# Layer norm, attention and feed-forward on one core: the kernel's own planner lays its steps out in parts, with nine tries for each

## The chip, the cores and the metric

The kernel runs on one core of a Trainium2 chip. A core has five engines that run their own instruction streams in order and meet through semaphores: TensorE (PE) for matrix products, VectorE (DVE), ScalarE (ACT) and GpSimd (POOL) for element work, and SyncE (SP), which here issues most of the DMAs. The metric is the device time of one execution in microseconds, the median of the runs shown.

## The reference

For 16 sequences of 512 tokens with 512 features, a layer norm feeds two branches, and both are added to the input:

```python
xn = _layernorm(x, axis=-1)
x = x + _L0_attn_ref(xn, w_qkv, b_qkv, w_out, b_out) + _L0_ffn_ref(xn, gate_w, up_w, down_w, gate_s, up_s, down_s)

# attention: 16 heads of 32, causal
qkv = einsum('bsd,ed->bse', x, w_qkv) + b_qkv
scores = einsum('bhqd,bhkd->bhqk', q, k) / sqrt(32) + causal
out = einsum('bhqk,bhkd->bhqd', softmax(scores), v)
return einsum('bsd,ed->bse', out, w_out) + b_out

# feed-forward: 1408 inner features, ternary weights with a scale for each row
g = einsum('th,ih->ti', xf, gate_w) * gate_s
u = einsum('th,ih->ti', xf, up_w) * up_s
return einsum('ti,hi->th', silu(g) * u, down_w) * down_s
```

## The kernel before

All is in float32 outside, and inside the operands of the large products are split into a high and a low float16 half (`xh` and `xl`, `qkh` and `qkl`, `hh` and `hl`, `oh` and `ol`), so that a product is made of two or three float16 products. The ternary weights of the feed-forward are held in fp8.

One batch is one sequence. Its heads come in four groups of four; a slot is one group of one batch, so there are 64 slots. For a slot PE makes the query and key projections (`qk`), the scores (`s`, L726) in runs, and the weighted sum of the values (`av`, L867). A run of scores fills the four PSUM banks of tag `s1`: run "3" has the last 128 queries against 512 keys, run "2, 0" the third and the first, run "1, 1" the second blocks of two slots. Names such as `s1_13` mean slot 1, block 3. For each of the four heads of a run DVE takes the row maximum with the mask (L765), ACT the exponential with its sum (L770); then ACT and DVE make the two halves `pq` (L797, L802), and a transposing DMA on SP's queue brings them to `pT` for the values product. The next run needs the four banks back, so it waits for the exponentials of the run before.

All other products of PE go through `mm_group` (one line, L359) in pieces of four matmuls of 512 columns, into three PSUM banks of tag `mm`: gate `g`, up `u`, down `dn`, `qk`, `v` and the output projection `op`. They fill the time between the score runs. Gate and up are evicted by ACT (tanh, L947), DVE (L951, L957), ACT again (`hh`, L960) and POOL (`hl`, L961).

The layer norm of the next batch runs beside this: four statistics steps on DVE (L484, L485), a seed of the inverse deviation on DVE (L491, L43, L44), Newton's steps on POOL (`newton_steps`, L50 to L53, twelve small operations, planned as one step of 2.9 us), the normalisation on DVE (`ln_norm`, L509, four steps planned at 0.5 us each), the high half on ACT (L522), the low half on POOL (L523), and transposing DMAs. DVE also carries small tests of the weights that are spread over the batches (L1046, L1053). At the end of the last batch, `av_step` with `split` makes the last slot's values product in two halves (`av`, `av_first`), each followed by its own eviction (L882, L900, L905), and the output products of the last group come after it.

Nothing of this is issued in the order in which it is written. Each piece is a `Step` with an engine, a duration estimated by hand, a latency, the tokens that it reads and writes, and for PE a key (where in the whole it should stand). `Plan.order` at the kernel's end lays all steps out in time, on the host, and the engines' streams are then issued in that order. Before the change it works so:

- `layout` goes from start to end. For each engine it lists the steps that can begin, with their start times; PE takes the earliest (among equals one that keeps the array's mode, then the smallest key), the others the earliest, and among equals the one with the smallest deadline `late`. If taking it would make a more urgent step late that comes free within WINDOW = 0.5 us, they wait for that one. The earliest choice over all engines is put into the plan.
- A change between wide, row-tiled and column-tiled products on PE costs SWITCH = 0.095 us in the layout.
- `deadlines` goes back through a finished layout and gives each step its latest end, from what needs it, from the buffer that it keeps, and for PE from its place in a row of PE steps without gaps.
- `order(6)` does this six times and takes the layout that ends first.

Of the kernel before, what the change touches and what calls it, by code (L numbers as in the profile page):

```python
# [2 lines left out]

# [54 lines left out]
SWITCH, LANDING = 0.095, 1.4  # L58
WINDOW = 0.5

BEGIN, FIRST_TURN = 0.75, 1.3

RUNS = 0.0, 0.17, 0.30, 0.64, 0.80
LAST_RUNS = 0.0, 0.14, 0.28, 0.42, 0.56
VERBOSE = False


# [26 lines left out]
class Plan:  # L94
# [30 lines left out]
        self.steps.append(st)  # L125
        return st

    def order(self, times):


        for n, st in enumerate(self.steps):
            st.n = n
            for d in st.deps:
                d.next.append(st)
        best = None
        for _ in range(times):
            done = self.layout()
            if done is None:
                break
            end = max(st.end for st in done)  # L140
            if best is None or end < best[0]:
                best = end, done, [(st.start, st.end) for st in done]
            if VERBOSE: print("pass", end)
            self.deadlines(done)
        for st, (t0, t1) in zip(*best[1:]) if best else ():
            st.start, st.end = t0, t1
        assert best, "no step can start"
        return best[1]

    def tiles(self):  # L150
        return dict.fromkeys(t for st in self.steps for t in st.tiles)
# [1 line left out]
    def deadlines(self, done):  # L153
        rings = {}
        for t in self.tiles():
            rings.setdefault(t.tag, {})[t.index] = t
        after = {}
        for ring in rings.values():
            for k, t in ring.items():
                if k >= t.bufs:  # L160
                    first = min(t.users, key=lambda u: u.start)
                    for u in ring[k - t.bufs].users:
                        after.setdefault(u, []).append(first)
        total, at = max(st.end for st in done), {}
        t = next(st.start for st in done if st.eng == "PE")
        for st in done:
            if st.eng == "PE":
                at[st] = t
                t += st.dur
        for st in done[::-1]:  # L170
            late = [x.late - st.lat * (x.eng != st.eng or st.dma) for x in st.next]
            late += [x.late - st.lat for x in after.get(st, ())]
            spent = st.lat + LANDING if st.dma else st.dur
            st.late = min([total] + late) - spent
            if st.eng == "PE":
                st.late = min(st.late, at[st])

    def layout(self):
        for st in self.steps:
            st.left, st.end = len(st.deps), None  # L180
            for t in st.tiles:
                t.index = None
        free = dict.fromkeys(self.ENGINES, BEGIN)
        ready = {e: [] for e in self.ENGINES}
        made, done, dma, mode = {}, [], FIRST_TURN, "wide"
        keys = sorted((s.key, s.n) for s in self.steps if s.eng == "PE")[::-1]

        def begin(st):

            t, more = st.at, {}  # L190
            if st.behind and st.behind.end is None:
                return None
            for b in st.tiles:
                if b.index is None:
                    l = made.setdefault(b.tag, [])
                    k = len(l) + more.get(b.tag, 0) - b.bufs
                    more[b.tag] = more.get(b.tag, 0) + 1
                    if k >= 0:
                        for u in l[k].users:
                            if u.end is None:  # L200
                                return None
                            t = max(t, u.end)
            return t

        def release(st):
            st.at = max([d.end - d.lat * (d.eng == st.eng and not d.dma) for d in st.deps], default=0.0)
            if st.late is None or first:
                st.late = st.at + st.slack
            ready[st.eng].append(st)

        first = all(st.late is None for st in self.steps)
        for st in self.steps:
            if not st.left:
                release(st)
        while len(done) < len(self.steps):
            best = None
            while keys and self.steps[keys[-1][1]].end is not None:
                keys.pop()
            for e in self.ENGINES:
                cands = [(max(t, free[e]), st) for t, st in ((begin(st), st) for st in ready[e]) if t is not None]  # L220
                if e == "PE":

                    cands = [
                        c for c in cands
                        if c[1].key <= keys[-1][0] + AHEAD or all(b.index is not None for b in c[1].tiles)
                    ]
                if not cands:
                    continue
                t0 = min(c[0] for c in cands)
                now = [c[1] for c in cands if c[0] <= t0 + 1e-6]  # L230
                if e == "PE":
                    st = min(now, key=lambda s: (s.mode == "wide" != mode, s.key, s.n))
                else:
                    st = min(now, key=lambda s: (s.late, s.n))
                    if not first:

                        t1, soon = min(cands, key=lambda c: (c[1].late + (c[0] > t0 + WINDOW) * 1e6, c[1].n))
                        if t0 + st.dur > max(soon.late, t1) and soon.late < st.late:
                            t0, st = t1, soon
                if best is None or t0 < best[0]:  # L240
                    best = t0, st
            if best is None:

                return None
            t, st = best
            ready[st.eng].remove(st)
            for b in st.tiles:
                if b.index is None:
                    b.index = len(made[b.tag])
                    made[b.tag].append(b)  # L250
            st.start = t
            free[st.eng] = t + st.dur
            st.end = t + st.dur + st.lat
            if st.eng == "PE":
                if st.mode != mode:
                    free["PE"] += SWITCH
                    st.end += SWITCH
                mode = st.leaves
            if st.dma:
                dma = max(dma, t) + st.lat  # L260
                st.end = dma + LANDING
            done.append(st)
            for x in st.next:
                x.left -= 1
                if not x.left:
                    release(x)
        return done


@with_exitstack  # L270
def fast_path(ctx, tc, good, x, wqkvT, bqk, bv, woT, bo, wgT, wuT, wdT, gs, us, dsc, out):
# [8 lines left out]
    plan = Plan()  # L280
# [47 lines left out]
    st = [dict() for _ in range(NB)]  # L328
# [852 lines left out]
    first, others, both = slice(0, P), slice(P, 512), slice(0, 512)  # L1181
# [21 lines left out]
    start = f.total  # L1203
    small_constants()
    load_ffn()
    for s in range(NSLOT):
        b, g = divmod(s, NG)
        if s % 2 == 0:
# [3 lines left out]
            last = s + 2 == NSLOT  # L1212
            for run, part in zip(runs, LAST_RUNS if last else RUNS):
                run.key = start + part * T
# [14 lines left out]
        k = s - 8 - s // 4 + 2  # L1229
# [8 lines left out]
        after = ends[tb](f, after)  # L1238
    f.place(start, f.total)

    done = plan.order(6)
    ET = mybir.EngineType
    with tc.manual_schedule(engines={ET.PE, ET.DVE, ET.Activation, ET.Pool, ET.SP}):
        for step in done:
# [155 lines left out]
def _program(tc, a, out):  # L1400
    nc = tc.nc
    args = [a[k] for k in ("x", "wqkvT", "bqk", "bv", "woT", "bo", "wgT", "wuT", "wdT", "gs", "us", "dsc")]
    with tc.tile_pool(name="flag", bufs=1) as fp:
        good = fp.tile([1, 1], I32, name="good")
        fast_path(tc, good, *args, out)
        n = nc.values_load(good, min_val=0, max_val=48)
        with tc.If(n < 48):
            general_path(tc, *args, out)
# [34 lines left out]
```

## Time and profile before

Three runs took 1861.12, 1862.27 and 1863.66 us. The profiled execution:

| | |
|---|---|
| median of the runs | 1862.27 us |
| the profiled execution's own time | 1861.75 us |
| its span, first to last instruction | 1860.0 us |
| granted TensorE clock, mean | 0.997 |
| PE matmuls, L359 `u`, `dn`, `g` | 1408 each |
| `qk`, `v`, `op` | 1536, 768, 768 |
| DVE L765 row maxima | 1024, 474.8 us |
| ACT L770 exponentials | 1024, 528.8 us |
| DVE L802 low halves of p | 384, 470.9 us |
| POOL L961 low halves of the gated values | 176, 240.1 us |
| DVE L509 normalisation | 60, 53.3 us, mean 940 ns |

The page of a profile gives, for each engine, the busy time and its share of the span; then the span in slices; then groups of equal instructions with busy time, mean length, and the idle time of the engine just before them with what ended it. "PE s L726 <- ACT p L770" reads: TensorE, about to write the tile `s` at line 726, waited for ScalarE's instruction that writes `p` at line 770. PEld is the loading of the stationary operand, which goes beside the products. In a timeline each row is a start, a length, an engine, a line and an operation, with the idle time before it in brackets. Matmul ends are modelled, so that matmuls overlap in these rows.

### The profile page before, as it was taken

The page shows a single profiled execution, that of the slowest core. Times are in us where ns is not written, and L with a number is a line of the kernel's source. Part 1 is how long each engine was busy: PE and PEld are TensorE (multiplying, and loading weights), DVE is VectorE, ACT ScalarE, POOL GpSimd, SP SyncE. Part 2 cuts the span into 40 slices and gives each one's busy share as a digit, 9 for nine tenths or more (in the row PEclk, how much of TensorE's full clock was granted, in tenths as well). Part 3 has the DMA queues.
Part 4 walks back from the last instruction along what each step waited for, and adds up shares of the span by engine and source line. Part 5 has one row for each costly group of instructions (what it writes and reads, how often), then busy time and mean ns, then how long its engine had stood idle before and what let it go on. Part 6 is the DMA issues. An engine that isn't in the chain of part 4 may idle for free.

```text
span 1860.0 us, 41219 instructions
## 1 busy us (share of the span) xinstructions
PE 1844.9 (99%) x15042; PEld 876.0 (47%) x15042; DVE 1547.7 (83%) x3662; ACT 1412.1 (76%) x3311; POOL 999.6 (54%) x931
## 2 busy tenths in 40 slices
PE   9999999999999999999999999999999999999998
PEld 4444444444444444444444444444444444444443
DVE  7879789798897978978789797897878878787777
ACT  7687887778777777777868777687777877778774
POOL 4654554555555454664646646456464564555543
PEclk9999999999999999999999999999999999999999
DMA  9877666667767656675686756767667665666556
GB/s 176 121 159 155 137 147 139 153 150 138 158 139 153 139 135 159 135 162 132 128 175 129 166 132 128 171 134 154 139 137 165 142 146 133 144 146 127 134 135 131
DMA packets 842548, 268.96 MB, mean 145 GB/s; under 512 B 806497, under 2 KB 813025, under 8 KB 842337
## 3 DMA queue, kind: packets, MB, share of 16 engines
q1 hardware_dynamic: 837296, 264.08, 65.3%
q0 software_dynamic: 5040, 2.16, 1.7%
q8 instruction: 120, 1.97, 0.5%
q14 instruction: 92, 0.75, 0.1%
HBM read 55.59 MB, written 16.78 MB: 39 GB/s over the span
## 4 chain that ended last, share of the span: by engine, by line
PE 94%; DVE 3%; ACT 2%; issue 1%; POOL 1%; DVEq 0%; ACTq 0%; POOLq 0%
PE qk L359 17%; PE u L359 16%; PE dn L359 16%; PE g L359 15%; PE v L359 9%; PE op L359 9%; PE s L726 6%; PE av L867 6%; DVE pq L802 1%; ACT p L770 1%; PE warm L628 1%; DVE s L765 1%; ACT pq L797 0%; DVE xc L509 0%; DVE ft L957 0%
## 5 line engine op out<-in xcount | busy, mean ns | idle before, releaser
L770 ACT ACTIVATE p<-s,negm 128x512 f32<-128x512 f32 (+3 forms) x1024 | 528.8, 526 | 217.6 <-DVE negm L765 216.4
L765 DVE CUSTOM_DVE_ANT_0 s<-s,mask 128x512 f32<-128x512 f32 (+3 forms) x1024 | 474.8, 515 | 116.2 <-PE s L726 108.4
L802 DVE SCALAR_TENSOR_TENSOR pq<-p,pq 128x1024 f16<-128x1024 f32 (+1 forms) x384 | 470.9, 1247 | 37.8 <-ACT pq L797 30.2
L961 POOL TENSOR_TENSOR hl<-ft,hh 128x512 f16<-128x512 f32 x176 | 240.1, 1366 | 248.3 <-ACT hh L960 245.6
L797 ACT ACTIVATE pq<-p 128x1024 f16<-128x1024 f32 (+1 forms) x384 | 339.8, 914 | 3.0
L359 PE MATMUL u<-xh,wu 128*128 128x512 f16 x704 | 267.4, 380 | 1.1 <-DVE ft L951 1.1
L359 PE MATMUL dn<-wd,hh 128*128 128x512 fp8e4 x704 | 267.2, 380 | 0.0
L359 PE MATMUL g<-xh,wg 128*128 128x512 f16 x704 | 267.0, 379 | 0.1
L359 PE MATMUL dn<-wd,hl 128*128 128x512 fp8e4 x704 | 266.8, 379 | 0.0
L359 PE MATMUL g<-xl,wg 128*128 128x512 f16 x704 | 266.8, 379 | 0.0
L359 PE MATMUL u<-xl,wu 128*128 128x512 f16 x704 | 266.8, 379 | 0.0
L668 POOL TENSOR_TENSOR qkl<-qkt,qkh 128x512 f16<-128x512 f32 x128 | 168.7, 1320 | 121.6 <-ACT qkh L666 114.1
L359 PEld LDWEIGHTS <-wg 128*128 128x128 fp8e4 x1408 | 136.0, 98 | 168.5 <-issue 7.0
L359 PEld LDWEIGHTS <-wu 128*128 128x128 fp8e4 x1408 | 133.1, 98 | 162.0 <-issue 5.4
L770 ACT ACTIVATION_READ_ACCUMULATOR p<-s,negm 128x1 f32 x1024 | 208.0, 203 | 0.0
L957 DVE SCALAR_TENSOR_TENSOR ft<-u,gu_c,ft 128x512 f32<-128x512 f32 x176 | 132.0, 750 | 37.9 <-PE u L359 29.9
L889 POOL TENSOR_SCALAR Rs<-Rs,bv_c 128x512 f32<-128x512 f32 x63 | 101.3, 1608 | 106.8 <-DVE Rs L882 104.1
L359 PEld LDWEIGHTS <-wq_h 128*128 128x128 f16 x1024 | 99.3, 98 | 124.2 <-issue 8.1
L947 ACT ACTIVATE ft<-g,gt_c 128x512 f32<-128x512 f32 x176 | 120.6, 685 | 43.6 <-PE g L359 40.8
L663 ACT ACTIVATE qkt<-qk,bqk_c 128x512 f32<-128x512 f32 x128 | 87.9, 688 | 84.9 <-PE qk L359 82.8
L951 DVE SCALAR_TENSOR_TENSOR ft<-ft,g 128x512 f32<-128x512 f32 x176 | 119.9, 681 | 38.4 <-ACT ft L947 33.9
L765 DVE DVE_READ_ACCUMULATOR2_ANT negm<- 128x1 f32 x1024 | 142.6, 139 | 0.0
(143 smaller groups left out, 3194.2 us busy)
## 6 DMA issues: line engine op xcount, KB each, us to landing
xc<-in_x SPq DMA_DIRECT2D x64, 256.0 KB, 4.2
xr<-in_x SPq DMA_DIRECT2D x64, 256.0 KB, 2.9
out<-y SPq DMA_DIRECT2D x64, 256.0 KB, 2.3
pT<-pq SPq DMA_TRANSPOSE x384, 3.7
exact<-in_wdT SPq DMA_DIRECT2D x11, 256.0 KB, 2.8
exact<-in_wgT SPq DMA_DIRECT2D x8, 256.0 KB, 2.9
exact<-in_wuT SPq DMA_DIRECT2D x8, 256.0 KB, 2.9
wq<-in_wqkvT SPq DMA_DIRECT2D x2, 768.0 KB, 8.2
```

Of the source, the lines that this page charges most:

```text
L359: nc.tensor.matmul(ps(), l, r, start=(first + k == 0), stop=(first + k == n - 1))
L668: "POOL", gps(512), lambda: nc.gpsimd.tensor_tensor(l(), t(), h(), ALU.subtract),
L726: nc.tensor.matmul(pss[j]()[:, off[u] : off[u] + n], q()[rows, i * P : (i + 1) * P], k()[rows, 0:n], start=(x == 0), stop=(x == 2), tile_p ...
L765: nc.vector.tensor_tensor_reduce(sc, sc, mask[:, 512 - n :], -(2.0 ** -7), 3e38, ALU.add, ALU.min, negm()[:, m : m + 1])
L770: nc.scalar.activation(exps(u).rearrange("p (k j) q -> p k j q", j=4)[:, :, j, :], part().rearrange("p (k q) -> p k q", q=P), AF.Exp, bias ...
L797: "ACT", 0.2 + 0.00085 * n, lambda src=src, half=half: nc.scalar.mul(half(0), src(), 2.0 ** 15),
L802: lambda src=src, half=half: nc.vector.scalar_tensor_tensor(half(1), src(), 2.0 ** 15, half(0), ALU.mult, ALU.subtract),
L867: nc.tensor.matmul(t()[j * 32 : (j + 1) * 32, col + q0 : col + 256], v()[:, k0, f : f + 32], pT[side][:, k0, j, z, q0:256], start=((side, ...
L947: "ACT", act(512) + 0.1, lambda: nc.scalar.activation(t(), pg(), AF.Tanh, scale=gt_c[:, ic : ic + 1]),
L951: "DVE", dve(512), lambda: nc.vector.scalar_tensor_tensor(t(), t(), 1.0, pg(), ALU.add, ALU.mult),
L957: lambda: nc.vector.scalar_tensor_tensor(t(), pu(), gu_c[:, ic : ic + 1], t(), ALU.mult, ALU.mult),
L961: add("POOL", gps(512), lambda: nc.gpsimd.tensor_tensor(hl(), t(), hh(), ALU.subtract), r=[t, hh], w=[hl])
```

## The change

The steps, their durations, their keys and their tokens stay as they are; what `Plan.order` does with them changes. The call becomes `plan.order(6, 8)`.

- The six whole layouts are made as before, but of the best one the deadlines are kept rather than the places.
- Then the plan is laid out once more in parts of PART = 60 PE steps. From the state at the start of a part, nine layouts are tried, each for 120 PE steps: one with the deadlines as they are and eight with every deadline put off by its own random amount of 0 to NOISE = 4 us (the generator has a fixed seed). The put-off deadlines decide on the engines other than PE alone.
- Of the nine the one with the smallest loss is kept for 60 PE steps, and the next part begins there. The loss is PE's idle time in the layout, and TIGHT = 0.02 times the time by which PE steps find their input less than ROOM = 0.8 us old.
- In `deadlines`, PE's row of steps without gaps now has the mode switches in it.
- `layout` is cut into `begin` (the state), `release`, `save`, `restore` and `go`, so that it can be stopped and taken up again.

The core of the diff:

```diff
+PART, NOISE, ROOM, TIGHT = 60, 4.0, 0.8, 0.02
...
-    def order(self, times):
+    def order(self, times, tries):
...
-        for _ in range(times):
-            done = self.layout()
-            if done is None:
+        for n in range(times):
+            lates = [st.late for st in self.steps]
+            state = self.begin(lates, n == 0)
+            if self.go(state, len(self.steps)) is None:
                 break
-            end = max(st.end for st in done)
+            end = max(st.end for st in self.steps)
             if best is None or end < best[0]:
-                best = end, done, [(st.start, st.end) for st in done]
+                best = end, [st.late for st in self.steps]
             if VERBOSE: print("pass", end)
-            self.deadlines(done)
-        for st, (t0, t1) in zip(*best[1:]) if best else ():
-            st.start, st.end = t0, t1
+            self.deadlines(state["done"])
         assert best, "no step can start"
-        return best[1]
+        rng = random.Random(1)
+        state = self.begin(best[1], False)
+        count, total = 0, sum(st.eng == "PE" for st in self.steps)
+        puts = [None] * len(self.steps)
+        while count < total:
+            saved, found = self.save(state), None
+            for k in range(tries + 1):
+                put = [rng.uniform(0, NOISE) if k else 0.0 for _ in self.steps]
+                state = self.restore(saved)
+                state["put"] = put
+                lost = self.go(state, count + 2 * PART)
+                if lost is not None and (found is None or lost < found[0] - 1e-6):
+                    found = lost, put
+            assert found, "no step can start"
+            state = self.restore(saved)
+            state["put"] = found[1]
+            count += PART
+            self.go(state, count)
+            if VERBOSE: print("part", count, found[0])
+        self.go(state, len(self.steps) + 1)
+        return state["done"]
...
-        total, at = max(st.end for st in done), {}
+        total, at, was = max(st.end for st in done), {}, "wide"
...
                 at[st] = t
-                t += st.dur
+                t += st.dur + SWITCH * (st.mode != was)
+                was = st.leaves
...
+        late = (lambda s: s.late + put[s.n]) if put else (lambda s: s.late)
...
-                    st = min(now, key=lambda s: (s.late, s.n))
+                    st = min(now, key=lambda s: (late(s), s.n))
                     if not first:
 
-                        t1, soon = min(cands, key=lambda c: (c[1].late + (c[0] > t0 + WINDOW) * 1e6, c[1].n))
-                        if t0 + st.dur > max(soon.late, t1) and soon.late < st.late:
+                        t1, soon = min(cands, key=lambda c: (late(c[1]) + (c[0] > t0 + WINDOW) * 1e6, c[1].n))
+                        if t0 + st.dur > max(late(soon), t1) and late(soon) < late(st):
                             t0, st = t1, soon
...
+                switch = SWITCH * (st.mode != state["mode"])
+                free["PE"] += switch
+                st.end += switch
+                state["mode"] = st.leaves
+                state["turns"] += 1
+                state["busy"] += st.dur + switch
+
+                state["tight"] += max(0.0, ROOM - (t - st.at))
...
-        return done
+        return free["PE"] - state["busy"] + TIGHT * state["tight"]
...
-    done = plan.order(6)
+    done = plan.order(6, 8)
```

More of the change, by code (lines that the diff above doesn't have):

```diff
@@ L1 @@
 import math
+import random
 from contextlib import ExitStack
@@ L176, in deadlines, with begin @@
                 st.late = min(st.late, at[st])
-    def layout(self):
-        for st in self.steps:
-            st.left, st.end = len(st.deps), None
+    def begin(self, lates, first):
+        for st, late in zip(self.steps, lates):
+            st.left, st.end, st.late = len(st.deps), None, late
             for t in st.tiles:
                 t.index = None
[L183 to L186, printed above, removed]
+        state = dict(
+            first=first, put=None, free=dict.fromkeys(self.ENGINES, BEGIN), ready={e: [] for e in self.ENGINES},
+            made={}, done=[], dma=FIRST_TURN, mode="wide", turns=0, busy=0.0, tight=0.0,
+            keys=sorted((s.key, s.n) for s in self.steps if s.eng == "PE")[::-1],
+        )
+        for st in self.steps:
+            if not st.left:
+                self.release(state, st)
+        return state
@@ new lines, in release, with save @@
+    def release(self, state, st):
+        st.at = max([d.end - d.lat * (d.eng == st.eng and not d.dma) for d in st.deps], default=0.0)
+        if st.late is None or state["first"]:
+            st.late = st.at + st.slack
+        state["ready"][st.eng].append(st)
+    def save(self, state):
+        return (
+            dict(state, free=dict(state["free"]), ready={e: list(l) for e, l in state["ready"].items()},
+                 made={t: list(l) for t, l in state["made"].items()}, done=list(state["done"]), keys=list(state["keys"])),
+            [(st.left, st.end, getattr(st, "start", None), getattr(st, "at", None)) for st in self.steps],
+            [(t, t.index) for t in self.tiles()],
+        )
@@ new lines, in restore, with go @@
+    def restore(self, saved):
+        state, steps, tiles = saved
+        for st, (st.left, st.end, st.start, st.at) in zip(self.steps, steps):
+            pass
+        for t, t.index in tiles:
+            pass
+        return dict(
+            state, free=dict(state["free"]), ready={e: list(l) for e, l in state["ready"].items()},
+            made={t: list(l) for t, l in state["made"].items()}, done=list(state["done"]), keys=list(state["keys"]),
+        )
+    def go(self, state, turns):
+        free, ready, made, done, keys, put = (state[k] for k in ("free", "ready", "made", "done", "keys", "put"))
+        first = state["first"]
+        late = (lambda s: s.late + put[s.n]) if put else (lambda s: s.late)
@@ L203, in begin @@
             return t
[L205 to L215, printed above, removed]
+        while len(done) < len(self.steps) and state["turns"] < turns:
             best = None
@@ L231, in layout @@
                 if e == "PE":
-                    st = min(now, key=lambda s: (s.mode == "wide" != mode, s.key, s.n))
+                    st = min(now, key=lambda s: (s.mode == "wide" != state["mode"], s.key, s.n))
                 else:
-                    st = min(now, key=lambda s: (s.late, s.n))
+                    st = min(now, key=lambda s: (late(s), s.n))
                     if not first:
-                        t1, soon = min(cands, key=lambda c: (c[1].late + (c[0] > t0 + WINDOW) * 1e6, c[1].n))
-                        if t0 + st.dur > max(soon.late, t1) and soon.late < st.late:
+                        t1, soon = min(cands, key=lambda c: (late(c[1]) + (c[0] > t0 + WINDOW) * 1e6, c[1].n))
+                        if t0 + st.dur > max(late(soon), t1) and late(soon) < late(st):
                             t0, st = t1, soon
@@ L254, in layout @@
             if st.eng == "PE":
[L255 to L258, printed above, removed]
+                switch = SWITCH * (st.mode != state["mode"])
[5 more added lines that the diff above has]
+                state["tight"] += max(0.0, ROOM - (t - st.at))
             if st.dma:
-                dma = max(dma, t) + st.lat
-                st.end = dma + LANDING
+                state["dma"] = max(state["dma"], t) + st.lat
+                st.end = state["dma"] + LANDING
             done.append(st)
@@ L265, in layout @@
                 if not x.left:
-                    release(x)
-        return done
+                    self.release(state, x)
+        return free["PE"] - state["busy"] + TIGHT * state["tight"]
 @with_exitstack
```

## The prediction

> **What bounds the kernel now.** I read the first part of the page, then PE's own waits, then busy time by windows of one batch, then the timeline at the few places where PE stood still.
>
> ```profile
> PE 1844.9 (99%) x15042; PEld 876.0 (47%) x15042; DVE 1547.7 (83%) x3662; ACT 1412.1 (76%) x3311; POOL 999.6 (54%) x931
> ```
> PE is busy for 1844.9 of 1860.0 us. A busy PE need not be a full PE, so the next look is at the distance between matmul starts:
>
> ```profile
> 137.63 0.38 PE L359 MATMUL u<-xh,wu 128*128 128x512 f16 x1
> 137.85 0.38 PE L359 MATMUL u<-xl,wu 128*128 128x512 f16 x1
> 138.06 0.38 PE L359 MATMUL u<-xh,wu 128*128 128x512 f16 x1
> 138.28 0.38 PE L359 MATMUL u<-xl,wu 128*128 128x512 f16 x1
> 138.78 0.38 PE L359 MATMUL g<-xh,wg 128*128 128x512 f16 x1
> ```
> Columns: start, length, engine, line. A wide matmul starts every 0.216 us although each is shown 0.38 long; so a wait up to 0.16 us is invisible in the busy time, and the last step (0.50 us) hides a wait of 0.29. Here the Trainium skill ("Perfetto Trace Analysis", section Identifying the Most-Contended Engine) warns that matmul busy share is a bad measure and that LDWEIGHTS share and MFU are the ones to read. By that rule 47% of PEld would leave half of PE to win. The rows decide otherwise: a load of 98 ns in a step of 216 ns is 45%, so 47% is what a PE without gaps shows in this kernel. A better order can win the gaps alone. Where are they?
>
> ```profile
> PE s L726 <- ACT p L770: 4.5, 5, 3.7
> PE warm L628 <- POOL vmin L314: 1.5, 1, 1.5
> PE u L359 <- DVE ft L951: 1.1, 2, 0.6
> PE op L359 <- ACT oh L900: 1.1, 1, 1.1
> ```
> (in total, times, longest.) And by windows of 114.15 us, one batch each:
>
> ```profile
> 114.15:228.30 114.15, 114.02 (x935) 53.96 (x934) 95.44 (x221) 88.30 (x210) 63.89 (x57) 1.00 0.74 149
> 342.45:456.60 114.15, 113.51 (x935) 53.77 (x933) 99.47 (x232) 88.62 (x208) 62.01 (x54) 1.00 0.68 144
> 570.75:684.90 114.15, 114.15 (x938) 54.24 (x937) 98.49 (x232) 87.61 (x207) 59.63 (x56) 1.00 0.65 146
> 1369.80:1483.95 114.15, 114.15 (x938) 54.22 (x937) 95.90 (x229) 87.79 (x207) 62.04 (x56) 1.00 0.65 146
> ```
> After the span and PE come PEld, DVE, ACT, POOL, the granted clock, DMA. From 570 us on PE has no idle time and the clock is full: eleven batches are at PE's floor. The gaps stand in the first five batches and at the end. Reading start to start (what exceeds the usual step of the same pair of matmuls): one stall of 5.9 us at 67 to 73 us; 0.24, 0.29, 0.33, 0.54, 0.80 and 0.63 us at 96, 139, 149, 319, 371 and 485 us; 0.23 at 1186 us, together **3.1**; and 1.1 before the last products. **10.1 us, 0.54% of the span, is all that an order can give.** The warm-up's 1.5 and the 6.7 us after the last matmul (1853.3 to 1860.0) are outside the plan's reach.
>
> The large stall is the one to understand:
>
> ```profile
> 63.56 5.91 DVE L509 TENSOR_SCALAR xc<-xc,mv,ln_y 128x512 f32<-128x512 f32 x4 [3.11 <-POOL ln_y L53]
> ```
> ```profile
> 70.17 0.69 ACT L770 ACTIVATE p<-s,negm 128x512 f32<-128x512 f32 x1 [4.01 <-DVE negm L765]
> ```
> ```profile
> 71.00 0.47 PE L726 MATMUL s<-qkh,qkh 32*128 32x384 f16 x1 [3.72 <-ACT p L770]
> ```
> DVE stood 3.11 us for the inverse deviation from POOL (12 small operations, 59.3 to 63.5), then four normalisations took 5.9 us. The plan's source has 2.9 us for the former and 0.5 for each of the latter. The row maxima (L765) stand behind them, the exponentials behind these, and the score run needs all four banks back.
>
> **The change, part by part.** It adds and removes no work: counted in the two built programs, the order and not the number of the matmuls differs. What it costs is what the new order makes wait.
>
> *Fewer turns of PE's mode.* PE's row of modes has 163 wide stretches, 160 score runs and 65 products before, 162, 160 and 64 after. A step from a wide matmul to a score costs 311 ns against 216: 0.1 us each way, **-0.2**.
>
> *The end.* Before, the two halves of the last values product stand apart: 1846.3 to 1847.5 and 1848.75 to 1849.4, and the first output product that needs them waits 1.07 us for DVE, then ACT. After, both stand together, ahead of some 19 output products of the other groups: 19 x 0.216 = 4.1 us that cover the chain of 1.1 us. The transposes that feed them have 19.6 us from the start of their scores (before: 17.8), the second half 20.8 (20.2), so nothing new is late: **-1.1**.
>
> *The stall at 67 us.* DVE's order there is the same in both: seed, one low half (L802, 1.2), vmin, the four L509, then the four row maxima. One of three statistics steps (0.8 us) that stood just before the seed went to an idle place 25 us earlier; but ACT now has a tanh (0.6) between the exponentials, and POOL has three 1.2 us operations ready right behind the deviation where before it had one and DMA issues. **-0.5**, between -2 and +1.5. The stall stays.
>
> *The small early waits, 3.1 us.* From the second batch on the orders differ everywhere, so these places no longer exist. The choice among nine layouts counts, beside the plan's idle PE, steps whose input is ready less than 0.8 us ahead (ROOM). That is just the size of these waits. I take half: **-1.5**, between -3.1 and 0.
>
> *New waits.* PE's deadlines now carry the mode switches. Before they ran ahead by 0.095 us at each of some 320 turns, 30 us at the end, so that late in the plan DVE and ACT always took the most urgent work; now they may fill in. In eleven of the fifteen batches (4 to 8 and 10 to 15) the four L509 now stand right ahead of the row maxima of a four-block run, some five DVE operations behind the seed; in the settled batches before they stood behind the row maxima of both next runs. What is queued behind is what stalled at 67 us. Worked out for batch 8, times from the start of its predecessor's value projection on PE: the fourth value tile ends at 10.4; its copy on ACT (0.62) and low half on DVE (0.6) end at 12.0; L1053 (0.7) at 12.7; the deviation from POOL comes 3.3 to 4.2 us after the seed at 8.9, so L509 starts at 13.0. The trace's four L509 take 53.3/15 = 3.55 us; with one L1011 (0.6) the maxima start at 17.2. From the first maximum to the score matmul that the last exponential releases the trace has 3.6 us (69.4 to 73.0): 20.8, and PE comes there at 22.4: **1.6 us left**.
>
> Here a rule speaks against the change. The Trainium skill ("SBUF — State Buffer", section Who interferes with whom) says that DVE and GpSimd share one port pair, held for an instruction's whole length: the later one blocks fully; `tensor_scalar` is among the DVE operations concerned. The trace agrees: L509 takes 0.53 us when POOL is quiet and 1.35 to 1.46 in 22 of 60, such as one from 872.73 to 874.10 that ends with POOL's L668 at 873.82; the worst quartet is the 5.91 above. The plan knows nothing of it. By the rule the quartet waits for both POOL operations that are ready there, L851 (1.22) and L523 (1.26): 4 x 0.53 + 2.5 = 4.6, and 0.6 us is left. By the worst row, 5.9, DVE is 0.7 us late in each of eleven batches: +7.7. I take the mean row, which leaves no stall there, and for what the plan doesn't know elsewhere **+1.0**, between 0 and +7.7: in the eleven quiet batches of before the unplanned lengths cost only 0.23.
>
> Sum against the profiled execution's own 1861.75 us (span 1860.0 and 1.75 around it): -0.2 - 1.1 - 0.5 - 1.5 + 1.0 = -2.3, so 1859.45. The median of the runs, 1862.27, lies 0.5 above that execution: **1860.0**.
>
> **Rivals.** *The 67 us stall closes too* (0.22). For it: the earlier statistics, other POOL work behind the deviation; against it: the same DVE order up to the maxima. With most of it gone: 1860.0 - 5 = 1855; with all gaps gone 1862.3 - 10 = 1852.
> *The normalisation block stalls PE in most batches* (0.18), the case on the other side. Place: L509 ahead of L765, eleven times; price 0.7 us each at a quartet of 5.9; it decides from a quartet of 5.2 us on. Then 1860.0 - 1.0 + 7.7 = 1866.7. For it: the lock, and that the plan's deadlines no longer rush. Against it: all these places need the worst quartet, and only one of 15 had it.
> *The order changes nothing* (0.10): what goes in one batch comes back in another, 1861.5 to 1863. For it: eleven batches have no gap to give.
> *The forecast* (0.50): 1857.5 to 1862.5.
>
> **How the numbers follow.** From 0.2% (3.7 us) a measurement tells a difference from none. Faster: the first rival nearly whole (0.20) and the forecast's lower edge (0.12). Slower: most of the third case (0.16) and a little for a place that I didn't work out. The range goes to 1854, which takes in most of a closed stall, and to 1867, the eleven small ones.
>
> **What would show it.** PE waits of L726 for L770: right if one of about 3.7 us at 67 us remains and little else; wrong by the first rival if it is gone; by the second if L726 waits once in each batch, with L509 ahead of L765 on DVE. The wait of L359 `op` for `oh` must be gone. Windows past 570 us should keep PE at 114.15; a batch longer than that is the second rival's sign. The forecast fails if the span moves by more than 4 us either way.

## The result, and the profile after

Four runs of the changed kernel took 1886.53 to 1890.57 us, median **1888.68 us**; the kernel before, run beside them, 1862.03. The ratio is 1.0142 [1.0127, 1.0157]: 26.7 us slower, where 2.3 us faster was forecast. The profiled execution spans 1887.1 us, 27.1 more than before.

The engines' row of the changed kernel's page, in the same columns as before:

```profile
PE 1852.7 (98%) x15042; PEld 877.1 (46%) x15042; DVE 1579.1 (84%) x3662; ACT 1396.4 (74%) x3311; POOL 1022.2 (54%) x931
```
The instruction counts are the same. PE's busy time grew by 7.8 us only, and 34.4 us of the span have no matmul at all (15.1 before). The granted clock is 0.999, so PE is not slower; it stands. Note DVE: the same 3662 instructions are busy for **31.4 us more** than before. An order alone should not change that.

What PE waited for in the changed kernel, all rows of the view (L1009 is the old L951, L828 the old L770, L784 the old L726):

```profile
PE u L417 <- DVE ft L1009: 14.0, 15, 1.8
PE s L784 <- ACT p L828: 6.6, 13, 1.6
PE s L784 <- POOL qkl L726: 1.9, 4, 0.8
PE warm L686 <- POOL vmin L372: 1.5, 1, 1.5
PE qk L417 <- DVE y L1069: 1.4, 2, 0.7
PE qk L417 <- DVE ft L1009: 0.7, 2, 0.4
PE v L417 <- DVE ft L1009: 0.2, 1, 0.2
PE g L417 <- DVE ft L1015: 0.2, 1, 0.2
```
The output product's wait for `oh` is gone, as forecast. The scores waited five times for the exponentials before, once for 3.7 us; now 13 times, never over 1.6. Largest now is a wait that took 1.1 us in all before: an up product `u` needs a PSUM bank of tag `mm`, and its last reader is DVE's L1009, the gated product of an earlier `g`. Since busy rows hide up to 0.16 us a matmul, I took the starts again: from 16 us on, the excess over the usual steps was 11.3 us before and 36.4 after, 25.1 of the span's 27.1. Of the 36.4, `u` for L1009 is some 16.5 and scores for L828 10.3, of which 3.8 are the old stall at 67 us.

Three of the settled batches, where PE had 114.15 of 114.15 us before (columns as in the prediction's windows):

```profile
684.90:799.05 114.15, 110.84 (x863) 52.02 (x853) 95.17 (x222) 83.88 (x205) 64.16 (x55) 1.00 0.65 143
799.05:913.20 114.15, 110.72 (x912) 52.06 (x911) 94.66 (x216) 82.62 (x195) 59.60 (x52) 1.00 0.59 135
1255.65:1369.80 114.15, 111.58 (x903) 52.77 (x901) 94.37 (x219) 82.75 (x200) 58.74 (x54) 1.00 0.69 141
```
(matmul counts are lower partly because fewer fit, partly because a few records are missing; the time is what counts here.) By starts, the windows past 570 us hold 0.6 to 5.1 us of stall each, where before only two held 0.2. The loss is spread, not one event.

One such place, first on DVE (start, length, line; idle time before in brackets):

```profile
426.89 0.55 DVE L1104 TENSOR_REDUCE ranges<-exact 128x1 f32<-128x384 f32 x1 [1.25 <-DMA exact<-in_wgT]
427.48 0.87 DVE L1111 SCALAR_TENSOR_TENSOR exact<-exact,wg 128x384 f32<-128x384 f32 x1
...
428.28 3.32 DVE L860 SCALAR_TENSOR_TENSOR pq<-p,pq 128x1024 f16<-128x1024 f32 x2
431.52 0.55 DVE L823 CUSTOM_DVE_ANT_0 s<-s,mask 128x384 f32<-128x384 f32 x1
...
432.51 0.68 DVE L1009 SCALAR_TENSOR_TENSOR ft<-ft,g 128x512 f32<-128x512 f32 x1
433.30 0.75 DVE L1015 SCALAR_TENSOR_TENSOR ft<-u,gu_c,ft 128x512 f32<-128x512 f32 x1
```
then what GpSimd did meanwhile, and PE:

```profile
428.23 1.16 POOL L581 TENSOR_TENSOR xnl<-xc,xnh 128x512 f16<-128x512 f32 x1 [0.30 <-ACT xnh L580]
```
```profile
431.75 0.38 PE L417 MATMUL g<-xl,wg 128*128 128x512 f16 x1
433.24 0.38 PE L417 MATMUL u<-xh,wu 128*128 128x512 f16 x1 [1.11 <-DVE ft L1009]
```
Read it from below. The step from 431.75 to 433.24 is 1.49 us in place of 0.216: PE is 1.27 us late. It waits for L1009, and the tanh that L1009 needs had ended on ACT at 429.4; L1009 stood in DVE's queue behind a weight test that waited 1.25 us for its data, and behind two low halves of `p` (L860). The plan's source gives such a low half 1.29 us, 2.58 for the two; they took 3.32, and the first began within 0.1 us of a GpSimd operation that reads SBUF. So two things that the plan doesn't know add up here: a late DMA, and DVE operations lengthened beside GpSimd. Which of them makes the 27 us is left to the experiments.

### The profile page after: what moved, and what is told of

The parts are those of the page before. It is cut to its first block, busy times and chain, and to the rows that moved or that the text cites. A ratio compares the mean times of both kernels' runs of the same rounds, so it can differ in the third digit from the quotient of the medians.

```text
span 1887.1 us, 41162 instructions
## 1 busy us (share of the span) xinstructions
PE 1852.7 (98%) x15042; PEld 877.1 (46%) x15042; DVE 1579.1 (84%) x3662; ACT 1396.4 (74%) x3311; POOL 1022.2 (54%) x931
## 4 chain that ended last, share of the span: by engine, by line
PE 65%; DVE 16%; ACT 7%; issue 5%; POOL 3%; DMA 3%; SPq 0%; DVEq 0%; ACTq 0%; POOLq 0%
PE dn L417 13%; PE qk L417 13%; PE u L417 10%; PE g L417 10%; DVE pq L860 5%; PE v L417 5%; PE op L417 5%; PE s L784 5%; DVE s L823 4%; PE av L925 4%; ACT p L828 4%; DVE ft L1009 2%; DVE xc L567 1%; ACT pq L855 1%; DVE negm L823 1%
## 5 line engine op out<-in xcount | busy, mean ns | idle before, releaser
L828 ACT ACTIVATE p<-s,negm 128x384 f32<-128x384 f32 (+3 forms) x1024 | 529.1, 528 | 244.7 <-DVE negm L823 242.2
L860 DVE SCALAR_TENSOR_TENSOR pq<-p,pq 128x1024 f16<-128x1024 f32 (+1 forms) x384 | 490.8, 1297 | 84.3 <-ACT pq L855 83.4
L823 DVE CUSTOM_DVE_ANT_0 s<-s,mask 128x384 f32<-128x384 f32 (+3 forms) x1024 | 476.2, 515 | 53.1 <-PE s L784 34.9
L726 POOL TENSOR_TENSOR qkl<-qkt,qkh 128x512 f16<-128x512 f32 x128 | 159.3, 1248 | 159.0 <-ACT qkh L724 151.1
L828 ACT ACTIVATION_READ_ACCUMULATOR p<-s,negm 128x1 f32 x1024 | 210.9, 206 | 0.0
L947 POOL TENSOR_SCALAR Rs<-Rs,bv_c 128x512 f32<-128x512 f32 x63 | 119.1, 1891 | 126.3 <-DVE Rs L940 117.1
L909 POOL TENSOR_TENSOR Rs<-R 128x512 f32<-128x512 f16 x64 | 82.9, 1295 | 127.6 <-DMA R<-rb 125.6
L1009 DVE SCALAR_TENSOR_TENSOR ft<-ft,g 128x512 f32<-128x512 f32 x176 | 119.7, 680 | 29.7 <-ACT ft L1005 29.5
L1018 ACT CAST hh<-ft 128x512 f16<-128x512 f32 x176 | 107.6, 617 | 37.2 <-DVE ft L1015 36.8
```

Source lines behind the costliest of these rows:

```text
L726: "POOL", gps(512), lambda: nc.gpsimd.tensor_tensor(l(), t(), h(), ALU.subtract),
L823: nc.vector.tensor_tensor_reduce(sc, sc, mask[:, 512 - n :], -(2.0 ** -7), 3e38, ALU.add, ALU.min, negm()[:, m : m + 1])
L828: nc.scalar.activation(exps(u).rearrange("p (k j) q -> p k j q", j=4)[:, :, j, :], part().rearrange("p (k q) -> p k q", q=P), AF.Exp, bias ...
L860: lambda src=src, half=half: nc.vector.scalar_tensor_tensor(half(1), src(), 2.0 ** 15, half(0), ALU.mult, ALU.subtract),
L947: "POOL", gps(n), lambda: nc.gpsimd.tensor_scalar(r(), r(), bias, None, ALU.add),
L1009: "DVE", dve(512), lambda: nc.vector.scalar_tensor_tensor(t(), t(), 1.0, pg(), ALU.add, ALU.mult),
```

## The experiments

**First: which part of the change.** Undoing both the put-off layouts and the corrected deadlines gives the instruction streams of before, so the cutting up of `layout` adds nothing of itself. One undone at a time:

```diff
-    done = plan.order(6, 8)
+    done = plan.order(6, 0)
```


> The changed kernel with no put-off deadlines (one layout for each part, the deadlines as they are); the corrected deadlines stay. Put-offs are the cause: back to 1866 us or less, TensorE waiting for DVE's L1009 in few places (under 3 us in total). The deadline correction is the cause: 1880 us or more, with the same waits as the changed kernel (14 us for L1009). Too short durations in the plan are the cause (a plan filled to the brim breaks on the chip): in between, 1870 to 1885, because the correction alone fills it as well.

```diff
-                t += st.dur + SWITCH * (st.mode != was)
+                t += st.dur
```


> The changed kernel with the old deadlines (no mode switches in TensorE's row), the nine tries stay. Put-offs are the cause: 1880 us or more. The deadline correction is the cause: 1866 us or less. Too short durations: 1870 to 1885.

Corrected deadlines without put-offs: 1859.5 us, 0.9986 [0.9979, 0.9993], a small gain. Put-offs with the old deadlines: 1863.1, 1.0006 [0.9997, 1.0015], no difference. Neither part costs anything alone with this seed; **together** they cost 1.4%. Both runs met the forecast of "this part is the cause", so each part is needed for the loss. The forecast for too short durations, a partial loss in each, failed: the durations matter below, but only where both parts are present. A smaller put-off lies between:

```diff
-PART, NOISE, ROOM, TIGHT = 60, 4.0, 0.8, 0.02
+PART, NOISE, ROOM, TIGHT = 60, 1.0, 0.8, 0.02
```


> The changed kernel with put-offs of at most 1 us instead of 4. Put-offs are the cause: about a quarter to a half of the loss, 1868 to 1876 us. The deadline correction or too short durations are the cause: as the changed kernel, 1882 to 1890.

1872.19, 1.0056 [1.004, 1.0073], in the range forecast for put-offs as the cause.

**Is it one unlucky draw?** The same with another seed, and the seed with the old deadlines:

```diff
-        rng = random.Random(1)
+        rng = random.Random(2)
```


> The changed kernel with another seed for the put-offs, all else the same. If the 26 us come from what the put-offs do in general, 1875 to 1895 us with L1009 as TensorE's main wait. If seed 1 drew a bad lot, within 1858 to 1868.

> The old deadlines with nine tries and the other seed. If the early deadlines protect the plan from its put-offs: 1866 us or less. A draw: above 1870 as likely as not.

1898.1 (1.0188 [1.0171, 1.0205]) and 1866.42 (1.0019 [1.0012, 1.0026]). The first is 3 us above its forecast and the second at its limit. The loss is no accident of one seed, and the old deadlines guard against most of it with either. The pairs also give a measure that the rest needs: two seeds lie 9.4 us apart in the changed kernel and 3.3 with the old deadlines, so a single redrawn plan that is 10 us better shows little.

**Is it what the plan doesn't know?** The durations of four kinds of step were set to what the traces show:

```diff
-    gps = lambda n: 0.15 + 0.0022 * n
+    gps = lambda n: 0.27 + 0.0022 * n
-        add("POOL", 2.9, rstd, ...)
+        add("POOL", 3.9, rstd, ...)
-            "DVE", 0.5,          # L567
+            "DVE", 0.95,
-                    "DVE", 0.06 + 0.0012 * n,      # L860
+                    "DVE", 0.26 + 0.00113 * n,
```


> The changed kernel with four durations in the plan set to what the trace shows (L567 0.95 for 0.5, the Newton steps on GpSimd 3.9 for 2.9, GpSimd's 512 columns 1.40 for 1.28, L860 1.42 for 1.29 and 0.84 for 0.67). Too short durations are the cause: 1868 us or less, DVE's waits for GpSimd at L567 under 5 us (15.7 in the changed kernel). Put-offs or the deadline correction are the cause: 1878 us or more.

1861.05 us, 0.9997 [0.9988, 1.0006]: the 27 us are gone, with deadlines and put-offs as in the change. With the other seed:

> The four durations from the trace with the other seed (the changed kernel with that seed took 1898 us). Short durations are the cause: 1866 us or less. A draw of layouts: anywhere up to 1895, above 1870 as likely as not.

1859.36, 0.9979 [0.9969, 0.9988]; 39 us against the same seed without the durations. Two seeds that gain 27 and 39 us are far outside what a new draw moves. And with the durations but without put-offs:

> Corrected deadlines, the four durations from the trace, no put-offs. If short durations harm only a plan that is filled by put-offs: the same as the run without put-offs, 1858 to 1861. If they cost there too: 1852 to 1857.

1860.41, 0.999 [0.9981, 0.9999]. The durations thus matter only where the put-offs are; without them they change nothing that can be told (1859.5 before them). Halves of the edit, first the layer norm's two durations, then the other two:

> The changed kernel with two of the four durations set right, those of the layer norm (L567 0.95 for 0.5, Newton's steps 3.9 for 2.9). If the missing layer-norm time is what breaks the filled plan: 1868 us or less, DVE's wait for GpSimd at L567 under 4 us. If the port lock's lengthening of L860 and of GpSimd's work is: 1878 us or more.

> The other two durations alone (GpSimd's 512 columns 1.40 for 1.28; L860 1.42 for 1.29 and 0.84 for 0.67). If the lengthened L860 and GpSimd operations are what breaks the plan: 1868 us or less. If the layer norm is: 1878 us or more. If any shift of the durations draws another layout and the result is a lottery, both this and the run with the layer-norm durations fall anywhere between 1860 and 1890 and the run with another seed differs from 1888 as well.

1871.4 (1.0044 [1.0028, 1.0061]) and 1868.65 (1.0034 [1.002, 1.0048]). Each brings over half, and both miss the limits set for one pair as the only cause. As the plan is drawn anew each time, the shares of the two can't be taken from this.

The page of the kernel with set durations, with its largest wait of PE:

```profile
PE 1844.0 (99%) x15042; PEld 875.8 (47%) x15042; DVE 1584.1 (85%) x3662; ACT 1399.0 (75%) x3311; POOL 1014.9 (55%) x931
```
```profile
PE u L417 <- DVE ft L1009: 3.8, 4, 1.3
```
DVE is busy for 1584.1 us, *more* than in the changed kernel (1579.1), and PE doesn't mind. So lengthened DVE work does not cost PE time by itself; it costs where the plan laid out urgent work as if there were no lengthening.

**Is it GpSimd that lengthens DVE?** The three experiments that follow keep an order as it is (no new draw) and change only GpSimd's low halves `hl`, `qkl`, `xnl`: they are left out, and zeros are written in their place, so these kernels compute without those halves. With the order of the changed kernel, of the kernel before (as a control), and with the changed order again but three writes that last about as long as the subtraction did:

```diff
-        add("POOL", gps(512), lambda: nc.gpsimd.tensor_tensor(hl(), t(), hh(), ALU.subtract), r=[t, hh], w=[hl])
+        add("POOL", gps(512), lambda: nc.gpsimd.memset(hl(), 0.0), r=[t, hh], w=[hl])
```


> The changed kernel's own order, but the three low halves that GpSimd makes (hl, qkl, xnl) are left out: it writes zeros there, reads nothing and is done in about half the time. If what the plan doesn't know of GpSimd and the shared port (longer L860 and L567, late low halves) makes the stalls: 1866 us or less, TensorE's waits for L1009 under 4 us, L860 near 1.25 us in the mean. If DVE's own order makes them, whatever GpSimd does: 1880 us or more.

> The same edit to the kernel before, in its own order: the control. It has 10 us of stalls to lose, 6 of them behind the normalisation of the second batch: 1853 to 1860.

```diff
+    def write_long(t):
+        nc.gpsimd.memset(t, 0.0)
+        nc.gpsimd.memset(t, 0.0)
+        nc.gpsimd.memset(t[:, 0:256], 0.0)
```


> As the changed kernel with GpSimd's writes only, but each low half (left out, zeros as before) is written three times over, 512, 512 and 256 columns, about 1.35 us in all and without a read. If the reads that hold DVE break the plan: within 3 us of the run with short writes, 1856 to 1862, and L860 stays near 1.3 us. If GpSimd's own length does: 1875 us or more. Half and half: 1864 to 1874.

| kernel | us | ratio to before | DVE busy | POOL busy |
|---|---|---|---|---|
| changed order | 1888.68 | 1.0142 [1.0127, 1.0157] | 1579.1 | 1022.2 |
| changed order, short writes | 1858.36 | 0.9975 [0.9964, 0.9986] | 1498.5 | 703.8 |
| changed order, long writes | 1858.59 | 0.9975 [0.9966, 0.9985] | 1502.8 | 1012.6 |
| order of before, short writes | 1856.32 | 0.9965 [0.9951, 0.9979] | 1494.4 | 689.2 |

All three times lie in the ranges forecast for GpSimd's reads as the cause. The edit brings 30 us in the changed order and some 6 in the order of before; the two orders then lie within 2 us. Long writes do as well as short ones, so it isn't GpSimd's length. The groups of L860, changed kernel and then changed order with long writes (there at L865); after the count come busy time and mean ns:

```profile
L860 DVE SCALAR_TENSOR_TENSOR pq<-p,pq 128x1024 f16<-128x1024 f32 x256 | 364.5, 1430 | 76.7 <-ACT pq L855 75.9
L860 DVE SCALAR_TENSOR_TENSOR pq<-p,pq 128x512 f16<-128x512 f32 x128 | 129.1, 1032 | 7.6 <-ACT pq L855 7.5
```
```profile
L865 DVE SCALAR_TENSOR_TENSOR pq<-p,pq 128x1024 f16<-128x1024 f32 x256 | 332.8, 1306 | 79.0 <-ACT pq L860 78.3
L865 DVE SCALAR_TENSOR_TENSOR pq<-p,pq 128x512 f16<-128x512 f32 x128 | 103.0, 829 | 13.2 <-ACT pq L860 13.1
```
1430 ns falls to 1306 and 1032 to 829, with DVE's own instructions unchanged and GpSimd busy as long. The Trainium skill ("SBUF — State Buffer", section Who interferes with whom) says that a DVE instruction with two inputs in SBUF, as L860 is, contends with a GpSimd instruction that reads SBUF and not with one that only writes it. The traces agree, instruction by instruction. In the kernel with long writes, 72 of the 256 wide low halves ran beside GpSimd writes alone and took 1221 ns in the mean, never over 1226; 54 ran beside nothing and took 1222; 129 ran beside a GpSimd operation that still reads, 1390 in the mean and up to 2312. In the changed kernel 60 had GpSimd idle (1220) and 196 ran beside a reading one (1494). The undisturbed price is thus 1.22 us, and the plan's 1.29 is enough only for a low half that meets no read.

PE's waits in the kernel with long writes, the largest three rows:

```profile
PE s L789 <- ACT p L833: 3.4, 9, 0.8
PE warm L691 <- POOL vmin L377: 1.5, 1, 1.5
PE u L422 <- DVE ft L1014: 0.2, 1, 0.2
```
The wait of `u` falls from 14.0 to 0.2. One caveat: a write without reads also needs no input from ACT, so GpSimd's results can come earlier than the subtraction's. In the changed kernel PE's only direct wait for such a half was 1.9 us (`s` for `qkl`), ACT's was 0.9, and DVE had none, so this can hardly be the 30, but these runs don't exclude that it has a part.

**Is it the weight tests' late data?** They waited in the changed kernel (from DVE's waits):

```profile
DVE ranges L1104 <- DMA exact<-in_wuT: 9.8, 3, 4.0
DVE ranges L1104 <- DMA exact<-in_wdT: 8.2, 3, 4.7
```
With 1.7 for `in_wgT` 19.7 us of waiting, none of it before. The changed order was kept, and only these two steps put eight DVE steps later:

```diff
-    done = plan.order(6, 8)
+    done = put_later(plan.order(6, 8), 8)
```


> The changed kernel's own order on every engine, but DVE's two steps of each weight test (L1104, L1111) are put eight DVE steps later, so that they no longer stand and wait for their load ahead of L1009. If DVE standing for this load is the main part of the loss: DVE's 19.7 us of waits there go under 3, and the time falls by 10 to 15 us, to 1873 to 1878. If these waits only fill time that DVE has anyway: 1885 to 1890.

1884.87, 1.012 [1.0103, 1.0137]: 3.8 us, where a main part was forecast at 10 to 15. The tests no longer wait, and PE's waits of `u` for L1009 halve (14.0 to 6.9 us), but DVE's wait for GpSimd ahead of L567 grows from 15.7 to 21.0 and PE's for the exponentials from 6.6 to 8.2. And in the kernel with long writes these tests still wait 9.0 us and PE loses nothing. Waits that look as bad as these cost little while the rest of DVE has a margin.

**Is it the choice among the nine?** The loss counts, besides PE's idle time, how close inputs come. Without that term, a put-off layout must have less idle time to be kept: 8 of the 35 parts keep one in place of 31.

```diff
-PART, NOISE, ROOM, TIGHT = 60, 4.0, 0.8, 0.02
+PART, NOISE, ROOM, TIGHT = 60, 4.0, 0.8, 0.0
```


> The changed kernel with TIGHT 0, so that the loss of a part is TensorE's idle time in the plan alone; all else, put-offs of 4 us too, as it was. 8 of 35 parts then keep a put-off layout, instead of 31. If the room term, which counts steps that follow their own group's matmul and doesn't count the PSUM banks, is what lets harmful put-offs in: 1866 us or less. If put-offs that remove idle time from the plan do the harm: 1875 us or more.

1877.0, 1.0079 [1.0063, 1.0096]. By matmul starts, its 27 parts with the plain layout hold 8.2 us of stall, 0.3 each; its 8 put-off parts 16.0, 2.0 each (1.6 without the stall of the second batch). So the stalls stand mostly in the put-off parts. Then the room was measured from the last input *or* the last release of a PSUM bank by another engine, once with the change's durations and once with the set ones:

```diff
-                state["tight"] += max(0.0, ROOM - (t - st.at))
+                state["tight"] += max(0.0, ROOM - (t - given))
```


> The changed kernel with another measure of room: the time since the last input or PSUM bank that another engine gives, TensorE's own matmuls not counted. If the blindness of the room term to the banks is the cause: 1868 us or less, TensorE's waits for L1009 under 4 us in total (14.0 in the changed kernel). If a layout with put-offs breaks on the chip whatever room it has in the plan, because the plan's durations are short: 1875 us or more.

> The four durations from the trace and the room of the banks together, put-offs of 4 us. If the two causes add up: below the run with the real durations alone, 1853 to 1859. If the durations were all: 1860 to 1863.

1877.87 (1.0085 [1.0068, 1.0102]), and 1868.86 (1.0037 [1.0023, 1.0052]), which is 8 us worse than with the set durations alone and above both of its forecasts. That the loss looks at the wrong thing is not supported by this: one draw got better, one worse, both by about what a draw moves.

## Why the prediction was wrong

**The step that failed is *New waits*, +1.0 between 0 and +7.7**, and in it the part for "what the plan doesn't know elsewhere". The whole changed by +27.1 us of span, and 25.1 of it are stalls that starts show; with what the end and the 67 us stall gave back (1.1 and 1.8) this term, with the small early waits in it, measured some +28 to +30. Two things in it were wrong.

*The lock was priced at one line.* The rule that spoke against the change was weighed only at L509's four steps in front of the maxima. L860, the L802 of before, is 384 instructions with two inputs in SBUF against 60, and DVE's largest group beside the maxima; its 1406 and 929 ns stood in the trace of before, against 1.29 and 0.67 us in the plan's source:

```profile
L802 DVE SCALAR_TENSOR_TENSOR pq<-p,pq 128x1024 f16<-128x1024 f32 x256 | 358.2, 1406 | 35.5 <-ACT pq L797 28.9 <-DMA xc<-in_x 4.1 <-DMA xh<-xnh 0.7
L802 DVE SCALAR_TENSOR_TENSOR pq<-p,pq 128x512 f16<-128x512 f32 x128 | 114.9, 929 | 2.3 <-ACT pq L797 1.4
```
That comparison, made for every planned duration, would have shown 256 x 0.12 + 128 x 0.26 = some 64 us of DVE work that the plan doesn't know.

*The quiet batches were taken as proof.* "The unplanned lengths cost only 0.23" was true of the order of before, and the prediction carried it over. The runs show where it holds: with the too early deadlines kept, the put-offs cost 1 or 4 us (two seeds); with the corrected ones 27 or 35. The prediction had named this margin ("late in the plan DVE and ACT always took the most urgent work; now they may fill in"), and then valued its end at the same price as before. That margin's end alone costs nothing (1859.5 us without put-offs); the put-offs had to fill it as well.

**The second rival** had the lock and the end of the rush as its cause, which is right in part, and the right sign of it, windows below 114.15 us past 570. Its place carried next to nothing. In the eleven batches where the four steps of L567 (the L509 of before) stand ahead of the maxima, they took 3.56 to 4.18 us from first to last, below the 5.2 from which it decides; of PE's 13 waits for the exponentials four, of 0.18 to 0.35 us each, come within 6 us behind one of these blocks. So the mean row that the prediction took for this place was a fair one. Over half of the new stalls came by a chain that neither looked at, L1009 behind L860 and others, with a PSUM bank of tag `mm` held for it.

**What held.** *The end*: the wait for `oh` is gone. *Fewer turns* is too small to be told from the rest. *The stall at 67 us* stayed, on the same normalisation steps; PE's rows in the changed kernel:

```profile
68.81 0.32 PE L784 MATMUL s<-qkh,qkh 32*128 32x384 f16 x1 [1.62 <-ACT p L828]
69.48 0.32 PE L784 MATMUL s<-qkh,qkh 32*128 32x384 f16 x1 [0.35 <-ACT p L828]
70.72 0.32 PE L784 MATMUL s<-qkh,qkh 32*128 32x384 f16 x1 [0.93 <-ACT p L828]
71.39 0.32 PE L784 MATMUL s<-qkh,qkh 32*128 32x384 f16 x1 [0.35 <-ACT p L828]
```
By starts these lose 3.8 us (1.69, 0.51, 1.09, 0.51) where the scores of that run lost 5.6 before by the same count: -1.8, inside the -2 to +1.5 given, though the middle value was -0.5. In both kernels matmuls behind this stall were slow, which the prediction's count of gaps leaves out. One microsecond of each, before and then after (columns as in the windows, the granted clock third from the end):

```profile
75.00:76.00 1.00, 1.00 (x3) 0.29 (x2) 1.00 (x3) 1.00 (x2) 1.00 (x1) 0.50 0.07 16
74.00:75.00 1.00, 1.00 (x4) 0.30 (x2) 1.00 (x6) 0.99 (x2) 1.00 (x2) 0.50 0.87 69
```
The clock was granted at 0.50 there, a step of `qk` took 0.427 us instead of 0.216, and this added 1.6 us before and 1.7 after; PE is busy in these rows and loses all the same.

*The small early waits* were forecast to halve, because ROOM is of their size. From 114 to 571 us the excess went from 2.3 to 5.2: wrong in sign, for the same reason as the rest.

**The ceiling** of 10.1 us, without the slow matmuls above, is not contradicted by any run, and none came near it: the best complete kernels here, set durations with put-offs of the second seed (1859.36, 0.9979 [0.9969, 0.9988]) and corrected deadlines without put-offs (1859.5, 0.9986 [0.9979, 0.9993]), beat the kernel before by 2 to 4 us and can't be told from each other. The second is the smaller edit.

What stays open: how much each of the wrong durations carries, how exactly deadlines that are too early protect a plan with put-offs (no run looks inside that), and whether a term of the loss could replace right durations; each try of that draws a new plan, and one draw moves by up to some 10 us.

## What to carry to other kernels

A planner that searches among its own layouts spends whatever margin its model shows as idle, so before a search is added, compare each planned duration with its mean in the trace, group by group, beginning with the largest. Margins can sit in what looks like a mistake (here deadlines 0.095 us too early at each turn): correct it and the search only with durations that hold. And when an order is in question, test it with the order held fixed and one cost removed; here plans redrawn with another seed differed by up to 9.4 us.

## What the runs showed of the hardware

The same DVE instructions in the same order took 1579.1 us beside GpSimd's subtractions and 1502.8 beside GpSimd writes of nearly equal total length (GpSimd busy 1022.2 and 1012.6 us). So 76 us, 5% of DVE's time, hung on what the subtractions do beyond writing; 58 of them are L860's. The wide low half, an instruction with two inputs in SBUF, was untouched by writes: 1221 ns beside writes alone, 1222 beside nothing. The normalisation's `tensor_scalar` (L572 there, one such input) was not quite: in the same run it took 533 ns beside nothing (20 times), 717 beside writes alone (22) and 1422 beside reads (18).

In the order of before the short writes took only 53 us off (1547.7 to 1494.4), against 81 in the changed one. How often the two engines meet is itself decided by the order, which a fixed duration in a plan only holds on average.
